# Rings of tiles that rest for some slots before they are taken again, stores a slot later, and more tiles behind them, in a four-layer kernel

## The chip, the cores and the metric

The kernel runs on one core of one Trainium2 chip. The metric is the time of one execution on the device in microseconds (us). All data are float32.

## The reference, cut to what matters

Four images of 384 channels by 48 x 48 positions go through four layers, each on a group-normalised input and added back to it.

```python
x = x + L0(_gn(x), ...)   # in projection, causal convolution, selective scan
                          # (768 channels x 16 states), gate, out projection, layer norm
x = x + L1(_gn(x), ...)   # 1x1 product, 8x8 FFT filter, 3x3 depthwise, gelu gate, 1x1 product
x = x + L2(_gn(x), ...)   # 11x11 depthwise convolution with one kernel per channel
x = x + L3(_gn(x), ...)   # four experts; the routing coefficients come from all four images
...
hdn = relu(einsum('bchw,edc->ebdhw', x, w1) + b1)   # L3
y = einsum('ebdhw,eod->ebohw', hdn, w2) + b2
out = einsum('ebohw,ebhw->bohw', y, coef)
```

## The kernel before, in words

The spine of the program is the scan of layer 0, written out as a fixed order of **slots**. Each image has 480 slots, four images make 1,920, and each slot holds one scan instruction of 460 or 464 positions on DVE (line 966). The scan of slot u needs a decay from ACT (942), a drive `bu = u * B` from POOL (953) and is followed by a product with `C` on DVE (986) or on POOL (995); PE turns the products and adds them up (886). `B` and `C` are rows that SP broadcasts from DRAM to 128 partitions (`spread`, 930): one `B` and one `C` for every two slots, into three and four tiles, so that a broadcast for a later pair of slots is queued only some five slots ahead of its first reader.

Everything else is cut into **tasks**: Python generators that stop at each `yield` and say on what kind of engine the next step runs. In each slot, `Lane.step` goes over the active tasks of a lane in three phases (`act`; then `pe`, `dve`, `pool`; then `late`) and lets each advance by one step at most. What a step emits stands at that place in the fixed order of its engine's queue. A `pe` step also has a weight, and a meter of PE time per slot holds steps back. There are four lanes: `aux` (layer 0's own projections, gates, the residual and the next chunk's load), `start` (layer 0's z of images 2 and 3, made early, during image 0), `one` (layers 1 and 2 and the router's scores of the image before: `later`), `two` (the experts of layer 3: `experts`). `later(b)` starts at slot 42 of image b+1, and `experts(b)` only when `later(b)` and `experts(b-1)` have ended. What is left of the experts of image 2, and layers 1 to 3 of image 3, follow after the last scan; `all_experts` (lines 1850 and 1867) ends the program.

A **ring** (`Ring`) mirrors a pool of n tiles in this order: `take` gives the next tile, `done` marks one as free, and a step that needs a tile isn't emitted until the one n takes before is marked. Where a tile is stored by a DMA, the program marks it when the store is *queued*. The tile framework adds the true dependency: a load into that tile waits on SP until the store has landed. SP issues its DMAs strictly in the order of the program, so all that is queued behind a waiting DMA on SP, the broadcasts of `B` and `C` too, waits as well.

An expert block (144 positions, one of four experts) runs so: `load3` (1737, 1740) queues the loads of `xe`, and for experts 1 to 3 of the running sum `ye`, then lets three slots pass; `block` then has the steps hidden product `ph` (PE), relu `hr` (ACT), second product `pout` (PE), sum (DVE, 1782 or 1785), and the store (1791) one slot after the sum. For expert 0 the sum is put into the `xe` tile and stored from there. In the scans there are two `xe`, two `ye`, one `hr` and one tile of weights; after the scans 3, 3, 3 and 2. In layer 2, `windows` adds a band's sum to the tile `xb`, of which there are two, and stores it (1582) a slot later; `load_band` (1513) fetches the next one.

Of the kernel before, what the change touches and what calls it, by code (L numbers as in the profile page):

```python
# [16 lines left out]
P = 128  # L17
# [11 lines left out]
NE = 4  # L29
# [12 lines left out]


class Ring:


    def __init__(self, make, n):
        self.make, self.n, self.read = make, n, []

    def free(self, k=1):  # L50
        return all(self.read[: max(0, len(self.read) + k - self.n)])

# [5 lines left out]
    def done(self, k):  # L58
        self.read[k] = True

# [34 lines left out]
class Lane:  # L95
# [6 lines left out]

    def step(self, phase, slot, at=0):
        for task in self.active:
            if task.ended:
                continue
            kind, weight, ring, when = task.next
            if PHASE.get(kind, 1) != phase or task.after > slot:
                continue
            if weight and self.bound and self.meter.value + weight > self.meter.limit:  # L110
                continue
            if (ring and not ring[0].free(ring[1])) or (when and not when()):
                continue
            self.meter.value += weight
            task.move(slot)
        self.active = [t for t in self.active if not t.ended]
        while (
            self.queue and len(self.active) < self.width and self.queue[0].at <= max(at, slot)
            and all(t.ended for t in self.queue[0].needs)
        ):  # L120
            task = self.queue.pop(0)
            task.move()
            if not task.ended:
                self.active.append(task)
# [18 lines left out]
def tile_layers(ctx: ExitStack, tc: tile.TileContext, a: dict, out: bass.AP):  # L143
# [21 lines left out]
    gsel = const("gsel", [P, CT, GROUPS], per_channel(a["c_gsel"]))  # L165
    gexp = const("gexp", [GROUPS, C], a["c_gexp"])
    neghalf = cp.tile([P, TT], F32, name="neghalf")
# [7 lines left out]
    def group_norm(st, bank, mean, rstd, name):  # L175

        mv = small.tile([P, CT, 2], F32, name=f"mv{name}", tag="mv")
        for ct in range(CT):
            nc.vector.bn_aggr(mv[:, ct, :], st[:, ct].rearrange("p k s -> p (k s)"))

        def to_groups(src, n, what):
            ps = bank(f"g{what}{name}")
            for ct in range(CT):
                nc.tensor.matmul(
                    ps[:GROUPS, :n], lhsT=gsel[:, ct, :], rhs=src(ct),
                    start=ct == 0, stop=ct == CT - 1,
                )
            return ps[:GROUPS, :n]

        def to_channels(src, n, what):  # L190
            ps = bank(f"c{what}{name}")
            for ct in range(CT):
                nc.tensor.matmul(
                    ps[:, n * ct : n * ct + n], lhsT=gexp[:, bass.ts(ct, P)], rhs=src,
                    start=True, stop=True,
                )
            return ps[:, : n * CT]

        grp = small.tile([GROUPS, 2], F32, name=f"grp{name}", tag="grp")
        nc.vector.tensor_copy(grp, to_groups(lambda ct: mv[:, ct, :], 2, "m"))  # L200
        nc.vector.tensor_copy(mean, to_channels(grp[:, 0:1], 1, "m"))
        dev = small.tile([P, CT], F32, name=f"dev{name}", tag="dev")
        nc.vector.tensor_sub(dev, mv[:, :, 0], mean)
        nc.vector.tensor_mul(dev, dev, dev)
        var = small.tile([GROUPS, 1], F32, name=f"var{name}", tag="var")
        nc.vector.scalar_tensor_tensor(
            var, to_groups(lambda ct: dev[:, ct : ct + 1], 1, "v"), GN_EPS, grp[:, 1:2],
            ALU.add, ALU.add,
        )
        nc.gpsimd.tensor_tensor(var, var, neghalf[:GROUPS, 0:1], ALU.pow)  # L210
        nc.vector.tensor_copy(rstd, to_channels(var, 1, "v"))

    def group_norm_steps(st, ring, mean, rstd, name):
# [15 lines left out]
        def to_channels(src, n, what):  # L229
            ps, k = ring.take(f"c{what}{name}")  # L230
            for ct in range(CT):
                nc.tensor.matmul(
                    ps[:, n * ct : n * ct + n], lhsT=gexp[:, bass.ts(ct, P)], rhs=src,
                    start=True, stop=True,
                )
            return ps[:, : n * CT], k
# [179 lines left out]
    with ExitStack() as first:  # L416
# [54 lines left out]

        stats0 = wp.tile([P, 2, CT, 2, 3, 6], F32, name="stats0")
        mean0 = wp.tile([P, NB, CT], F32, name="mean0")
# [85 lines left out]
        def scans(wk, mm, ring, meter, place, lanes, begin):  # L559
# [9 lines left out]
            def image_stats(b, ct, h):  # L569
# [4 lines left out]
                for k in range(3):  # L574
                    yield ("dve",)
                    nc.vector.bn_stats(stats0[:, b % 2, ct, h, k, :], t[:, bass.ts(k, LB)])

            def image_norm(b):
                yield from group_norm_steps(
                    stats0[:, b % 2].rearrange("p c h k s -> p c (h k) s"), ring,  # L580
                    mean0[:, b], rstd0[:, b], f"0_{b}",
                )
# [54 lines left out]
            def early_z(b, t, j):  # L637
# [21 lines left out]
                ring.done(r)  # L659
                yield ("pool",)  # L660
                nc.sync.dma_start(zd[b][bass.ts(j, P), bass.ds(starts[t], n)], z[:, :n])
# [514 lines left out]
            for tag, shape, n in (  # L1176
# [6 lines left out]
                    ),  # L1183
                    n,
                )
# [82 lines left out]
        def later(b, ring, accr):  # L1268
# [10 lines left out]

            def slots(tag, shape, n):  # L1280

                return Ring(
                    lambda name: d["wk"].tile(shape, F32, name=name, tag=tag, bufs=n), n
                )
# [10 lines left out]
            def begin1():  # L1295
                wk = d["wk"] = stack.enter_context(tc.tile_pool(name=f"l1_{b}", bufs=2))
                d["w_in"] = wk.tile([P, CT, C], F32, name=f"w_in1_{b}", tag="w_in", bufs=1)
                nc.sync.dma_start(d["w_in"], per_channel(a["L1_w_inT"]))
                w = d["w_out"] = wk.tile([P, 2, C], F32, name=f"w_out1_{b}", tag="w_out", bufs=1)
                nc.sync.dma_start(w[:, 0, :], a["L1_w_outT"][:P, :])  # L1300
                nc.sync.dma_start(w[64:P, 1, :], a["L1_w_outT"][P:, :])
                mean = small.tile([P, CT], F32, name=f"mean1_{b}", tag="mean")
# [90 lines left out]
            def finish_strip(hb):  # L1393
# [46 lines left out]
                for ct in range(CT):  # L1440
                    yield ("pe", 1.3, (ring, 1))
                    ps, r = ring.take(f"pb{b}_{hb}_{ct}")
                    nc.tensor.matmul(  # L1443
                        ps[:, :LB], lhsT=w[:, 0, bass.ts(ct, P)], rhs=act[:, 0, :],
                        start=True, stop=False,
                    )
                    nc.tensor.matmul(  # L1447
                        ps[:, :LB], lhsT=w[64:P, 1, bass.ts(ct, P)], rhs=act[64:P, 1, :],
                        start=False, stop=True,
# [27 lines left out]
            x2s = slots("x2", [P, BR * W], 4)  # L1477
            xbs = slots("xb", [P, max(BANDS) * W], 2)
            reps = slots("rep", [P, NBC, NP, BR, BC], 2)
# [67 lines left out]
            def windows(ct, k, r, first, last, final):  # L1547
# [26 lines left out]
                if last:  # L1574
# [5 lines left out]
                    nc.vector.bn_stats(stats3[b % 2][:, ct, k, :], x[:, :n])  # L1580
                    yield ("pool",)
                    nc.sync.dma_start(x3d[b][of_band(ct, k)], x[:, :n])
# [38 lines left out]

            xg = slots("xg", [P, CT, LB], 2)

# [64 lines left out]
        def experts(b, ring, rings):  # L1688
# [42 lines left out]
            def load3(s, e):  # L1731
                yield (
                    "pool", 0, None,
                    lambda: rings["xe"].free() and (not e or rings["ye"].free()),
                )
                x = take(("x", s, e), "xe", f"xe{b}_{s}_{e}")
                nc.sync.dma_start(x, strip(x3d[b], bass.ts(s, EB)))
                if e:
                    y = take(("y", s, e), "ye", f"ye{b}_{s}_{e}")
                    nc.sync.dma_start(y, strip(y3d, bass.ts(s, EB)))  # L1740
                yield from wait(3)

            def block(s, e):
# [33 lines left out]
                yield ("late",)  # L1777
                key = ("y" if e else "x", s, e)
                x = d[key][0]
                if e:  # L1780
                    y = x.rearrange("p c t -> p (c t)")
                    nc.vector.tensor_add(y, ps[:, : CT * EB], y)  # L1782
                else:
                    for m in range(CT):
                        nc.vector.scalar_tensor_tensor(
                            x[:, m, :], ps[:, bass.ts(m, EB)], b2_sum[:, m : m + 1],
                            x[:, m, :], ALU.add, ALU.add,
                        )
                ring.done(r)
                yield ("pool",)  # L1790
                nc.sync.dma_start(strip(out[b] if e == NE - 1 else y3d, bass.ts(s, EB)), x)
                done(key)

# [104 lines left out]

        def of_experts(pool, sizes):
            for tag, n in sizes.items():  # L1900
# [4 lines left out]
                    ),  # L1905
                    n,
                )
# [13 lines left out]
        def begin(b):  # L1921
# [9 lines left out]
            first.enter_context(tc.tile_pool(name="experts", bufs=2)),  # L1931
            {"we": 1, "xe": 2, "ye": 2, "hr": 1},
        )
        with (
# [6 lines left out]
            at = place[0]  # L1941
            while not all(ring.read):
                at += 1
# [5 lines left out]
        with (  # L1949
# [3 lines left out]
            holder[0], ring.n, accr.n = mm, 6, 2  # L1953
            of_experts(wk, {"we": 2, "xe": 3, "ye": 3, "hr": 3})

# [129 lines left out]
```

## Time and profile before

| | |
|---|---|
| median of 3 runs | 5400.23 us (5399.6 to 5402.55) |
| the profiled execution | 5405.14 us, span 5403.1 us |
| mean granted PE clock | 0.919 |
| PE, DVE, POOL, ACT busy | 86%, 75%, 62%, 55% |
| scans of layer 0 | about 85 to 4,512 us |
| rest of the experts of image 2, layers 1 and 2 of image 3 | about 4,512 to 5,060 us |
| scores and all experts of image 3 | about 5,060 to 5,403 us |

In the views, `<-` in the name of a group stands between what is written and what is read. In the waits, each line names who waited, for whom, the total in us, how often, and the longest. `SPq` is the issuing queue of SP: its waits are the times for which a DMA at the head of that queue held it.

### The profile page before, as it was taken

The page shows a single profiled execution, that of the slowest core. Times are in us where ns is not written, and L with a number is a line of the kernel's source. Part 1 is how long each engine was busy: PE and PEld are TensorE (multiplying, and loading weights), DVE is VectorE, ACT ScalarE, POOL GpSimd, SP SyncE. Part 2 cuts the span into 40 slices and gives each one's busy share as a digit, 9 for nine tenths or more (in the row PEclk, how much of TensorE's full clock was granted, in tenths as well). Part 3 has the DMA queues.
Part 4 walks back from the last instruction along what each step waited for, and adds up shares of the span by engine and source line. Part 5 has one row for each costly group of instructions (what it writes and reads, how often), then busy time and mean ns, then how long its engine had stood idle before and what let it go on. Part 6 is the DMA issues. An engine that isn't in the chain of part 4 may idle for free. (4 is left out here: it accounts for less than half of the span.)

```text
span 5403.1 us, 82006 instructions
## 1 busy us (share of the span) xinstructions
PE 4646.1 (86%) x27796; PEld 3666.7 (68%) x27796; DVE 4067.1 (75%) x5581; ACT 2989.0 (55%) x6632; POOL 3363.1 (62%) x3020
## 2 busy tenths in 40 slices
PE   5898877787768988888889988888799988999899
PEld 3555545454446766765668867665678877889799
DVE  5998899889997888889887778798987875452200
ACT  3566655565547765565567745565477653335321
POOL 3788778886677788876678678775677783000000
PEclk8898987788879999998899999998899999999899
DMA  4565545443344555655566565655566573543210
GB/s 152 172 187 175 178 128 150 129 143 120 111 127 131 148 165 157 191 161 147 149 172 178 161 200 155 173 146 149 154 182 174 158 213 115 175 138 105 64 27 23
DMA packets 648873, 794.36 MB, mean 147 GB/s; under 512 B 60149, under 2 KB 642661, under 8 KB 648062
## 3 DMA queue, kind: packets, MB, share of 16 engines
q1 hardware_dynamic: 638148, 787.38, 49.9%
q8 instruction: 221, 3.62, 0.3%
q10 hardware_dynamic: 10298, 1.67, 0.2%
q14 instruction: 206, 1.69, 0.1%
HBM read 685.04 MB, written 103.81 MB: 146 GB/s over the span
## 5 line engine op out<-in xcount | busy, mean ns | idle before, releaser
L953 POOL TENSOR_TENSOR bu<-u,B 128x460 f32<-128x460 f32 (+1 forms) x1920 | 2227.0, 1170 | 795.5 <-DVE g L966 349.8
L942 ACT ACTIVATE da<-dt,a_neg 128x460 f32<-128x460 f32 (+1 forms) x1920 | 1242.4, 648 | 310.6 <-DVE g L986 185.6
L886 PE MATMUL y<-ident,g 128*115 128x128 f32 (+1 forms) x7680 | 1111.3, 292 | 192.5 <-DVE g L986 114.8
L886 PEld LDWEIGHTS y<-ident,g 128*115 128x115 f32 (+1 forms) x7680 | 991.2, 183 | 400.4 <-DVE g L986 140.5
L995 POOL TENSOR_TENSOR g<-g,C 128x460 f32<-128x460 f32 (+1 forms) x885 | 1030.0, 1164 | 246.8 <-ACT carry L980 244.3
L966 DVE TENSOR_TENSOR_SCAN da<-da,carry,bu 128x460 f32<-128x460 f32 (+1 forms) x828 | 971.7, 1174 | 122.2 <-ACT da L942 76.7
L966 DVE TENSOR_TENSOR_SCAN g<-da,carry,bu 128x460 f32<-128x460 f32 (+1 forms) x708 | 819.8, 1167 | 57.7 <-issue 18.8
L986 DVE TENSOR_TENSOR g<-da,C 128x460 f32<-128x460 f32 (+1 forms) x1035 | 656.4, 634 | 175.7 <-DMA C<-bcd 62.0
L980 ACT COPY carry<-da 128x1 f32<-128x1 f32 x828 | 130.3, 157 | 760.5 <-DVE g L986 758.0
L1750 PE MATMUL pout<-hr,we 128*128 128x144 f32 x3456 | 485.0, 297 | 51.5 <-ACT hr L1766 37.8
L1750 PE MATMUL ph<-xe,we 128*128 128x144 f32 x3456 | 484.7, 298 | 33.6 <-DMA xe<-x3d 18.9
L1750 PEld LDWEIGHTS pout<-hr,we 128*128 128x128 f32 x3456 | 456.3, 197 | 75.3 <-ACT hr L1766 47.9
L1750 PEld LDWEIGHTS ph<-xe,we 128*128 128x128 f32 x3456 | 459.4, 199 | 51.5 <-DMA xe<-x3d 13.7
L1557 PE MATMUL pc<-band,row 128*128 128x162 f32 (+14 forms) x3456 | 451.3, 284 | 11.2 <-ACT row L1544 10.9
L1557 PEld LDWEIGHTS pc<-band,row 128*128 128x128 f32 x3456 | 440.0, 194 | 16.6 <-ACT row L1544 11.9
L749 PE MATMUL pin<-xch,w_inx 128*128 128x463 f32 (+2 forms) x720 | 344.8, 621 | 55.1 <-DMA xch<-in_x 32.3
L1415 DVE SCALAR_TENSOR_TENSOR dw<-pad,w_dw,dw 128x384 f32<-128x384 f32 x576 | 348.0, 615 | 20.4 <-ACT pad L1390 9.6
L1037 PE MATMUL po<-w_out,zs 128*115 128x384 f32 (+1 forms) x960 | 342.2, 499 | 14.7 <-DVE ye L1782 9.3
L1766 ACT ACTIVATE hr<-ph,nb 128x144 f32<-128x144 f32 x576 | 176.2, 376 | 279.2 <-PE ph L1750 278.4
L1524 ACT ACTIVATE rep<-x,br,wr 128x192 f32<-128x192 f32 x576 | 273.7, 540 | 4.2 <-issue 4.2
L768 DVE SCALAR_TENSOR_TENSOR xc<-pin,conv_w,xc 128x460 f32<-128x460 f32 (+1 forms) x360 | 249.2, 692 | 30.7 <-ACT xc L762 18.5
L749 PEld LDWEIGHTS pin<-xch,w_inx 128*128 128x128 f32 x720 | 143.8, 213 | 179.8 <-issue 136.3
(211 smaller groups left out, 5979.2 us busy)
## 6 DMA issues: line engine op xcount, KB each, us to landing
B<-bcd SPq DMA_DIRECT2D x768, 230.0 KB, 3.6
C<-bcd SPq DMA_DIRECT2D x768, 230.0 KB, 4.0
B<-bcd SPq DMA_DIRECT2D x192, 232.0 KB, 3.8
C<-bcd SPq DMA_DIRECT2D x192, 232.0 KB, 4.3
xe<-x3d SPq DMA_DIRECT2D x192, 216.0 KB, 2.8
ye<-y3d SPq DMA_DIRECT2D x144, 216.0 KB, 2.8
y3d<-ye SPq DMA_DIRECT2D x96, 216.0 KB, 2.2
xs<-x1d SPq DMA_DIRECT2D x24, 576.0 KB, 5.2
```

The lines of the kernel that those rows point to most:

```text
L749: nc.tensor.matmul(ps[:, lo : halo + n], lhsT=w_inx[:, k, bass.ts(j, P)], rhs=c["x"][:, k, lo : halo + n], start=k == 0, stop=k == CT - 1,)
L886: nc.tensor.matmul(c["y", m][:w, bass.ts(k, P)], lhsT=src[:, bass.ts(k, w)], rhs=ident, is_transpose=True, start=c["terms", m] == 1 and k ...
L942: nc.scalar.activation(da[:, :n], c["dt", p][:, m % 2, :n], AF.Exp, scale=a_neg[:, m, s : s + 1])
L953: nc.gpsimd.tensor_mul(bu[:, :n], c["u", p][:, m % 2, :n], live["B", u // 2][:, :n])
L966: nc.vector.tensor_tensor_scan(here[:, :n], da[:, :n], bu[:, :n], last if t else nil[:, 0:1], ALU.mult, ALU.add,)
L986: nc.vector.tensor_mul(live["g", u][:, :n], live["h", u][:, :n], live["C", u // 2][:, :n])
L995: nc.gpsimd.tensor_mul(g[:, :n], g[:, :n], live["C", u // 2][:, :n])
L1037: nc.tensor.matmul(ps[:w, :C], lhsT=c["zs"][:, m, bass.ts(k, w)], rhs=w_out0[:, m, :], start=m == 0, stop=m == MT - 1,)
L1415: nc.vector.scalar_tensor_tensor(v, src, w_dw[:, ct, k : k + 1], v, ALU.mult, ALU.add)
L1524: nc.scalar.activation(rep[:, :, n, :, :].rearrange("p g r c -> p r g c"), rows.rearrange("p (r g c) -> p r g c", r=BR, c=BC), AF.Identity ...
L1557: nc.tensor.matmul(d["acc2"][0][:, : BANDS[k] * W].rearrange("p (h w) -> p h w", w=W)[:, lo - edges[k] : hi - edges[k], xlo:xhi], lhsT=d[" ...
L1750: nc.tensor.matmul(ps[:, bass.ts(m, EB)], lhsT=w[:, k, bass.ts(m, P)], rhs=of[:, k, :], start=k == 0, stop=k == CT - 1,)
```

## The change

- `Ring` gets a number of slots, `rest`: a tile counts as free only `rest` slots after its `done`. The slot is kept in `CLOCK`, set by every `Lane.step`. The psum rings and most others rest for 0 slots.
- The experts' rings in the scans: `xe` 2 tiles resting 1 slot, `ye` three tiles (two before) resting 2. After the scans the sizes stay 3 and 3, without a rest.
- The sum of expert 0 goes to a `ye` tile and is stored from there; `load3` takes a `ye` for expert 0 too and lets two slots pass, not three. The experts' store is queued two slots after the sum, not one.
- Layer 2: `xb` 4 tiles resting 2 slots (2 tiles before), the store two slots after the sum. The scores' `xg` rest 1 slot.
- The early z: all its rings rest 2 slots, the store comes two slots after the copy.
- Room for the tiles: one `stats0` in place of two; the second part of layer 1's `w_out` (64 rows) moves into the unused partitions of the constant `gexp`, loaded once on ACT's queue instead of once per image on SP.
- In place stay the store of layer 0's residual (1095), the load of its next chunk (731) and the store of layer 1 (1457).

```diff
-    def __init__(self, make, n):
-        self.make, self.n, self.read = make, n, []
+    def __init__(self, make, n, rest=0):
+        self.make, self.n, self.read, self.rest = make, n, [], rest
     def free(self, k=1):
-        return all(self.read[: max(0, len(self.read) + k - self.n)])
+        return all(
+            v is not False and v + self.rest <= CLOCK[0]
+            for v in self.read[: max(0, len(self.read) + k - self.n)]
+        )
...
     def done(self, k):
-        self.read[k] = True
+        self.read[k] = CLOCK[0]
...
     def step(self, phase, slot, at=0):
+        CLOCK[0] = slot
...
-    gexp = const("gexp", [GROUPS, C], a["c_gexp"])
+    gexp = cp.tile([P, C], F32, name="gexp")
+    nc.sync.dma_start(gexp[:GROUPS, :], a["c_gexp"])
+    nc.scalar.dma_start(gexp[64:P, :], a["L1_w_outT"][P:, :])
...
# early_z
-                yield ("pool",)
+                yield from wait(2)
                 nc.sync.dma_start(zd[b][bass.ts(j, P), bass.ds(starts[t], n)], z[:, :n])
...
# later
-                nc.sync.dma_start(w[:, 0, :], a["L1_w_outT"][:P, :])
-                nc.sync.dma_start(w[64:P, 1, :], a["L1_w_outT"][P:, :])
+                nc.sync.dma_start(w, a["L1_w_outT"][:P, :])
...
-            xbs = slots("xb", [P, max(BANDS) * W], 2)
+            xbs = slots("xb", [P, max(BANDS) * W], 4, 2)
...
# windows
-                    yield ("pool",)
+                    yield from wait(2)
                     nc.sync.dma_start(x3d[b][of_band(ct, k)], x[:, :n])
...
-            xg = slots("xg", [P, CT, LB], 2)
+            xg = slots("xg", [P, CT, LB], 2, 1)
...
# experts: load3
-                    lambda: rings["xe"].free() and (not e or rings["ye"].free()),
+                    lambda: rings["xe"].free() and rings["ye"].free(),
...
+                y = take(("y", s, e), "ye", f"ye{b}_{s}_{e}")
                 if e:
-                    y = take(("y", s, e), "ye", f"ye{b}_{s}_{e}")
                     nc.sync.dma_start(y, strip(y3d, bass.ts(s, EB)))
-                yield from wait(3)
+                yield from wait(2)
...
# experts: block, expert 0
                         nc.vector.scalar_tensor_tensor(
-                            x[:, m, :], ps[:, bass.ts(m, EB)], b2_sum[:, m : m + 1],
+                            y[:, m, :], ps[:, bass.ts(m, EB)], b2_sum[:, m : m + 1],
                             x[:, m, :], ALU.add, ALU.add,
                         )
+                    done(("x", s, e))
                 ring.done(r)
-                yield ("pool",)
-                nc.sync.dma_start(strip(out[b] if e == NE - 1 else y3d, bass.ts(s, EB)), x)
-                done(key)
+                yield from wait(2)
+                nc.sync.dma_start(strip(out[b] if e == NE - 1 else y3d, bass.ts(s, EB)), y)
+                done(("y", s, e))
...
-            {"we": 1, "xe": 2, "ye": 2, "hr": 1},
+            {"we": 1, "xe": 2, "ye": 3, "hr": 1}, {"xe": 1, "ye": 2},
...
-            while not all(ring.read):
+            while not ring.free(ring.n):
```

More of the change, by code (lines that the diff above doesn't have):

```diff
@@ L41 @@
 LN_EPS = 1e-5
+CLOCK = [0]
 class Ring:
-    def __init__(self, make, n):
-        self.make, self.n, self.read = make, n, []
+    def __init__(self, make, n, rest=0):
+        self.make, self.n, self.read, self.rest = make, n, [], rest
     def free(self, k=1):
-        return all(self.read[: max(0, len(self.read) + k - self.n)])
+        return all(
+            v is not False and v + self.rest <= CLOCK[0]
+            for v in self.read[: max(0, len(self.read) + k - self.n)]
+        )
     def take(self, name):
@@ L193, in to_channels @@
                 nc.tensor.matmul(
-                    ps[:, n * ct : n * ct + n], lhsT=gexp[:, bass.ts(ct, P)], rhs=src,
+                    ps[:, n * ct : n * ct + n], lhsT=gexp[:GROUPS, bass.ts(ct, P)], rhs=src,
                     start=True, stop=True,
@@ L232, in to_channels @@
                 nc.tensor.matmul(
-                    ps[:, n * ct : n * ct + n], lhsT=gexp[:, bass.ts(ct, P)], rhs=src,
+                    ps[:, n * ct : n * ct + n], lhsT=gexp[:GROUPS, bass.ts(ct, P)], rhs=src,
                     start=True, stop=True,
@@ L470, in tile_layers @@
         nc.vector.tensor_reduce(b2_sum, b2_all.rearrange("p e c -> p c e"), AX.X, ALU.add)
-        stats0 = wp.tile([P, 2, CT, 2, 3, 6], F32, name="stats0")
+        stats0 = wp.tile([P, 1, CT, 2, 3, 6], F32, name="stats0")
         mean0 = wp.tile([P, NB, CT], F32, name="mean0")
@@ L575, in image_stats @@
                     yield ("dve",)
-                    nc.vector.bn_stats(stats0[:, b % 2, ct, h, k, :], t[:, bass.ts(k, LB)])
+                    nc.vector.bn_stats(stats0[:, 0, ct, h, k, :], t[:, bass.ts(k, LB)])
             def image_norm(b):
                 yield from group_norm_steps(
-                    stats0[:, b % 2].rearrange("p c h k s -> p c (h k) s"), ring,
+                    stats0[:, 0].rearrange("p c h k s -> p c (h k) s"), ring,
                     mean0[:, b], rstd0[:, b], f"0_{b}",
@@ L1183, in scans @@
                     ),
-                    n,
+                    n, 2,
                 )
@@ L1278, in put, with slots @@
                 tasks.append(task)
-            def slots(tag, shape, n):
+            def slots(tag, shape, n, rest=0):
                 return Ring(
-                    lambda name: d["wk"].tile(shape, F32, name=name, tag=tag, bufs=n), n
+                    lambda name: d["wk"].tile(shape, F32, name=name, tag=tag, bufs=n), n, rest
                 )
@@ L1298, in begin1 @@
                 nc.sync.dma_start(d["w_in"], per_channel(a["L1_w_inT"]))
-                w = d["w_out"] = wk.tile([P, 2, C], F32, name=f"w_out1_{b}", tag="w_out", bufs=1)
-                nc.sync.dma_start(w[:, 0, :], a["L1_w_outT"][:P, :])
-                nc.sync.dma_start(w[64:P, 1, :], a["L1_w_outT"][P:, :])
+                w = d["w_out"] = wk.tile([P, C], F32, name=f"w_out1_{b}", tag="w_out", bufs=1)
+                nc.sync.dma_start(w, a["L1_w_outT"][:P, :])
                 mean = small.tile([P, CT], F32, name=f"mean1_{b}", tag="mean")
@@ L1443, in finish_strip @@
                     nc.tensor.matmul(
-                        ps[:, :LB], lhsT=w[:, 0, bass.ts(ct, P)], rhs=act[:, 0, :],
+                        ps[:, :LB], lhsT=w[:, bass.ts(ct, P)], rhs=act[:, 0, :],
                         start=True, stop=False,
@@ L1447, in finish_strip @@
                     nc.tensor.matmul(
-                        ps[:, :LB], lhsT=w[64:P, 1, bass.ts(ct, P)], rhs=act[64:P, 1, :],
+                        ps[:, :LB], lhsT=gexp[64:P, bass.ts(ct, P)], rhs=act[64:P, 1, :],
                         start=False, stop=True,
@@ L1777, in block @@
                 yield ("late",)
-                key = ("y" if e else "x", s, e)
-                x = d[key][0]
+                y = d["y", s, e][0]
                 if e:
-                    y = x.rearrange("p c t -> p (c t)")
-                    nc.vector.tensor_add(y, ps[:, : CT * EB], y)
+                    of = y.rearrange("p c t -> p (c t)")
+                    nc.vector.tensor_add(of, ps[:, : CT * EB], of)
                 else:
@@ L1897, in tile_layers, with of_experts @@
         place = [0]
-        def of_experts(pool, sizes):
+        def of_experts(pool, sizes, rest):
             for tag, n in sizes.items():
@@ L1905, in of_experts @@
                     ),
-                    n,
+                    n, rest.get(tag, 0),
                 )
@@ L1953, in tile_layers @@
             holder[0], ring.n, accr.n = mm, 6, 2
-            of_experts(wk, {"we": 2, "xe": 3, "ye": 3, "hr": 3})
+            of_experts(wk, {"we": 2, "xe": 3, "ye": 3, "hr": 3}, {})
             one.queue += later(NB - 1, ring, accr)
```

## The prediction

> **What bounds the kernel now.** I read the page first, then SP's own waits, then DVE's waits, then the issuing queue of SP row by row, then engine times by stage. By the page no engine is the bound of the whole (PE 86%, DVE 75%), so the stages decide.
>
> SP's own waits (who, at which line, for what: total us, times, longest) show what the change is about:
>
> ```profile
> SPq L930 <- POOL bu L953: 1759.8, 649, 12.1
> ...
> SPq L1740 <- DMA y3d<-ye: 244.6, 92, 7.5
> SPq L1791 <- DVE ye L1782: 240.2, 91, 7.6
> SPq L1737 <- DMA y3d<-xe: 156.8, 47, 8.0
> SPq L1513 <- DMA x3d<-xb: 139.0, 52, 5.6
> SPq L1582 <- DVE xb L1578: 116.4, 43, 8.0
> SPq L1740 <- DMA out<-ye: 113.9, 39, 7.2
> ```
>
> The first line is the normal state: a broadcast of B waits until POOL has read the tile, so SP is in step. Lines 1740, 1737 and 1513 are loads into a tile whose store was queued just before and has not landed: 244.6 + 113.9 + 156.8 + 139.0 = 654 us of SP. Lines 1791 and 1582 are stores queued before DVE has made the sum. Who pays? DVE's and POOL's waits:
>
> ```profile
> DVE g L986 <- DMA C<-bcd: 62.0, 28, 6.1
> ...
> POOL bu L953 <- DMA B<-bcd: 98.2, 49, 7.2
> ```
>
> So of 654 us little reaches an engine: a broadcast is queued some five slots ahead. It does where the experts run beside bare scans; SP's queue there (start, duration):
>
> ```profile
> 4387.29 0.39 SPq L1791 DMA_DIRECT2D out<-ye  x1
> 4387.77 0.43 SPq L1737 DMA_DIRECT2D xe<-x3d  x1
> 4393.64 0.36 SPq L1740 DMA_DIRECT2D ye<-y3d  x1
> 4394.09 0.44 SPq L930 DMA_DIRECT2D B<-bcd  x1
> ...
> 4397.58 0.56 SPq L1737 DMA_DIRECT2D xe<-x3d  x1
> 4403.03 0.36 SPq L1740 DMA_DIRECT2D ye<-y3d  x1
> 4403.48 0.44 SPq L930 DMA_DIRECT2D B<-bcd  x1
> ```
>
> Each block the queue stands still for 5 us (4388.20 to 4393.64, 4398.14 to 4403.03), waiting for the store that it has just sent; then two pairs of broadcasts go out together, late. DVE's product at 4400.39 and that at 4409.31 each wait 1.67 us for C.
>
> By stage (us, busy PE, PEld, DVE, ACT, POOL, clock, DMA):
>
> ```profile
> 2080.00:2154.00 74.00, 67.11 (x484) 57.79 (x483) 64.19 (x91) 43.20 (x76) 60.02 (x54) 1.00 0.57 150
> 2700.00:2760.00 60.00, 48.23 (x319) 38.76 (x317) 56.75 (x84) 34.87 (x81) 44.34 (x41) 0.97 0.59 171
> 2880.00:2940.00 60.00, 59.02 (x428) 51.56 (x427) 46.10 (x58) 45.96 (x114) 47.61 (x43) 1.00 0.62 185
> 4600.00:4800.00 200.00, 197.03 (x1259) 167.15 (x1260) 101.89 (x188) 73.15 (x168) 0.77 (x4) 0.98 0.52 153
> ```
>
> Row 1, experts beside bare scans: nothing is full. Row 2, layer 1 beside experts: DVE 95%, so SP's waits cost next to nothing. Row 3, layer 2 beside experts: PE 98%. Row 4, after the scans: PE 98%, and each expert block still to do costs its own PE time.
>
> **A: SP's waits in the scans.** DVE's idle time ended by C is 62.0. POOL's waits for B pass to DVE in part: the view of tile B has 27.5 and 13.1 us of scans waiting behind them, 40.6. Sum 102.6. For each of these waits I took SP's rows of the 12 us before it and the longest standstill other than a broadcast's. For C: 28.1 us behind the ye load, 9.1 behind the xb load, 7.8 behind the xe load, so 45 of 62; 14.6 behind the next chunk's load (731), which stays. For B, 88% of POOL's waits stand behind these three loads: 36 of 40.6. Removable: 81 us. How much is realised? Bounds: 0 (PE or DVE takes the place at once) and 81. Most of the waits lie in stages like rows 1 and 3, half of which are full on PE; I take 40.
>
> Is a rest of two slots enough? A slot is 2.3 us (4,425 us of scans over 1,920), so two are 4.6. The DMA table gives a landing after 2.2 us for y3d<-ye and 4.5 for out<-ye, and the waits go up to 7.5. The Trainium skill ("DMA: Bandwidth & Descriptors", Anatomy of one DMA) has about 2.0 us fixed plus bytes over 436e3 per us: for the 221,184 bytes here an estimate of 2.5 us. By the page a rest of two slots covers every store and A's 81 us are all removable; by the trace out<-ye (48 of 144 ye stores) lands at the edge, and a part of its wait stays. The trace decides, another reason to take 40. The same section says that a DMA's semaphore wait happens on the issuing sequencer, as the rows above show; xe and xb rest or have two more tiles, so these should go to near zero.
>
> **B: the pace of the experts.** Before, an expert's ye (xe for expert 0) is held for 8 slots: load, three of wait, ph, relu, pout, sum, store, next take. Two tiles give a block every 4 slots; the trace agrees (y3d<-xe stores at 2131.34, 2140.29, 2148.04 and 2154.80, 7.8 us apart; 2.3 us x 4 is 9.2 at the mean slot, and these slots are shorter). After: load at 0, ph 3, pout 5, sum 6, store 8, free 10: three tiles give 3.33; for expert 0 xe is free at 7, two tiles give 3.5. The floor of hr is 3. So 12 to 17% faster where latency sets the pace; elsewhere the PE meter does.
>
> But experts(b) waits for later(b) too. The last scores of image 2 are loaded at 4372, the experts of image 1 end with a store at 4451, some 33 slots later (counted by scans). later becomes longer: a band's last window ends a slot later and the next band's first needs it, 15 bands, 15 slots, and some 3 for xg's rest. So the experts of image 2 can start at most 33 - 18 = 15 slots sooner, about 4 blocks at 3.5, plus one from the faster pace up to the scans' end: 5 blocks leave the tail. There a block costs 2 x 2.21 = 4.4 us (the chain has ph and pout at 2.21 for 18 matmuls). In the scans it costs what slots with experts take above slots with only scores: slots 864 to 912 took 88 us, 912 to 960 took 111; 0.48 us a slot, 1.9 a block. Gain 5 x (4.4 - 1.9) = 12. Bounds: 0, and 25 if the longer layer 2 costs no slot.
>
> **C: between the last scan and the tail** (4506 to 4590) expert 0's chain is store 4.2, xe load 2.7, ph, pout, sum. The store leaves it. PE was idle 3.0 of 60 and 11.7 of 60 us in the two rows from 4500; at most 15, I take 6.
>
> **D: what costs.** ph comes three slots after its load, not four: 2.3 us less lead. The load lands in 2.8 median, 9.1 at most; PE and its loader wait 18.9 and 20.7 us for xe now, and as the standstills that delay it go, I add 3 (0 to 15). The early z takes one slot more per task; 60 of them in a row fill 690 - 200 = 490 us now, 60 slots more end near 820, before their limit at slot 480 (1047 us): 0; SP's waits for the copy before that store (104 us) reach an engine with 2.3 + 2.6 us for C and B between 150 and 1100, so they give 3 at most. The w_out rows: one DMA more on ACT's queue at the start, 0.4 us, four fewer on SP. stats0: image 1's statistics come long after image 0's were used. Stores later on SP move past at most one pair of broadcasts and their neighbours; whoever waits for them (y3d, 16 blocks later; x3d for the scores, after the last band) is far, but for the last band, one slot.
>
> Sum: -40 - 12 - 6 + 3 = -55. Of the profiled execution, 5405.1 (its span and 2.0 around it): 5350. It stood 4.9 above the median, so 5345 for the median.
>
> **The rivals.** (1) *Slower: layer 2's extra slots.* If lane one loses more than the 33 slots of slack (18 by my count, the rest because experts that are ready more often take meter time from layers 1 and 2), the experts of image 2 start later than before, and each 3.5 slots push a block of 4.4 us into a tail that is 98% PE. At 60 slots: 27 / 3.5 = 8 blocks, +34 us, less 10 from A: 5424. For it: the meter is shared, and row 3 is full. Against: lane one is served first. (2) *No change:* A goes to PE and DVE at once (rows 2 and 3), B is eaten by layer 2: 5397. For it: of SP's 654 us at the three loads 81 reach DVE, an eighth. (3) *More:* all 81 are realised, B and C at their ends: 5405 - 81 - 25 - 15 - 5 = 5279. For it: in row 1 no engine is full, and SP's loop of store, landing, load is the only thing that repeats. (4) *It doesn't do what it says:* the stores land later than two slots and ye loads still stand: A 15 instead of 40, 5370; in the range.
>
> **How the numbers follow.** Main case with (4) 0.57, (3) 0.13, (2) 0.12, (1) 0.18. 0.2% is 11 us, about what a measurement can tell from no change. Faster 0.70, same 0.12, slower 0.18. The main case alone spans 5310 to 5385; with (3) and most of (1) the range is 5272 to 5424.
>
> **What would show it.** Right: SP's lines for 1740, 1737 and 1513 waiting for stores fall from 654 to below 150 us; DVE's waits for C from 62 to near 25 (the chunk's load remains); y3d stores of expert 0 every 3.5 slots; the last scan 40 to 50 us earlier, the tail 12 to 20 us shorter. Wrong: a last scan at the same time with these waits gone (rival 2), or later(2) ending after slot 1,890 and more than 59 blocks after the scans (rival 1).

## The result, and the profile after

The changed kernel takes 5353.4 us against 5399.9 (medians of 4 runs each): ratio 0.9917, 95% interval 0.990 to 0.9934. It is 46 us faster, where the prediction had 55. Its profiled execution took 5354.36 us, with a span of 5352.2. The lines of the code moved by 10 or 11: SP's broadcasts are now at line 941, `load3` at 1747 and 1750, the experts' store at 1801, xb's load and store at 1523 and 1592, the scan at 977, the product with C at 997.

SP's own waits in the changed kernel (who, where, for what: total us, times, longest):

```profile
SPq L941 <- POOL bu L964: 2376.2, 823, 11.8
...
SPq L1747 <- PE ph L1760: 153.3, 63, 9.2
SPq L1801 <- DVE ye L1791: 144.8, 74, 8.2
...
SPq L1592 <- DVE xb L1588: 67.5, 29, 10.8
...
SPq L1750 <- DMA y3d<-ye: 64.0, 37, 5.9
...
SPq L1750 <- DMA out<-ye: 19.9, 17, 2.9
...
SPq L1523 <- DMA x3d<-xb: 17.8, 11, 3.0
```

Loads that stand behind a store still under way cost SP 64.0 + 19.9 + 17.8 = 102 us, where they had cost 654, and SP waits longer in its normal state (first line, 1,760 before). Two stretches of its queue (start, duration). The first is from expert 3 of image 1, as the rows of before are, though beside the last scores and not beside bare scans; the second from expert 0 of image 2 beside bare scans, where a block loads no `ye`:

```profile
4331.02 0.44 SPq L1801 DMA_DIRECT2D out<-ye  x1
4332.70 0.33 SPq L941 DMA_DIRECT2D B<-bcd  x1
...
4333.56 0.42 SPq L1747 DMA_DIRECT2D xe<-x3d  x1
4336.14 0.37 SPq L1750 DMA_DIRECT2D ye<-y3d  x1
...
4447.10 0.37 SPq L1747 DMA_DIRECT2D xe<-x3d  x1
4447.52 0.49 SPq L1801 DMA_DIRECT2D y3d<-ye  x1
4448.45 0.33 SPq L941 DMA_DIRECT2D B<-bcd  x1
```

In the first stretch a load of `ye` still stands 2.2 us behind a store (4333.98 to 4336.14; in the rows of before it was 5), but a pair of broadcasts has gone out in between. In the second no load waits for the store, and a broadcast leaves 0.4 us after it. DVE's waits in the changed kernel:

```profile
DVE da L977 <- ACT da L953: 96.1, 78, 7.6
DVE g L997 <- PE y L897: 64.8, 43, 12.0
DVE da L977 <- ACT carry L991: 47.9, 18, 7.6
...
DVE g L997 <- DMA C<-bcd: 4.2, 3, 2.1
```

C is no cause of idle time any more (62.0 before, 4.2 now), and POOL's waits for B fell from 98.2 to 16.5. But the three lines above it have grown by 21 us together; before, they were:

```profile
DVE da L966 <- ACT da L942: 93.3, 66, 6.4
...
DVE g L986 <- PE y L886: 53.4, 36, 8.9
...
DVE da L966 <- ACT carry L980: 41.0, 16, 5.1
```

The 1,920th scan starts at 4515.3 us before and at 4508.5 after. So of 51 us of span only 7 were won in the scans, and 44 after them. The stretch after the last scan, before (first pair) and after (second pair; window, its length, busy PE, PEld, DVE, ACT, POOL):

```profile
4500.00:4560.00 60.00, 56.98 (x383) 49.09 (x382) 24.60 (x46) 15.98 (x39) 14.71 (x13) 1.00 0.29 81
4560.00:4620.00 60.00, 48.27 (x352) 46.48 (x351) 12.96 (x39) 16.59 (x40) 2.42 (x8) 0.86 0.59 176
```

```profile
4500.00:4560.00 60.00, 58.29 (x396) 50.62 (x395) 18.95 (x41) 15.73 (x39) 9.41 (x10) 1.00 0.34 99
4560.00:4620.00 60.00, 58.19 (x432) 53.40 (x431) 13.31 (x31) 20.11 (x50) 1.16 (x6) 1.00 0.86 268
```

PE's idle time there fell from 14.8 to 3.5 us. And by the last scan 139 of 192 expert blocks have been stored, 134 before.

That the waits for B and C went and yet the scans ended hardly sooner is what the experiments have to explain.

### The profile page after: what moved, and what is told of

It is laid out like the page before. It is cut to its first block, busy times and chain, and to the rows that moved or that the text cites. A ratio compares the mean times of both kernels' runs of the same rounds, so it can differ in the third digit from the quotient of the medians.

```text
span 5352.2 us, 81964 instructions
## 1 busy us (share of the span) xinstructions
PE 4643.7 (87%) x27796; PEld 3663.3 (68%) x27796; DVE 4069.8 (76%) x5581; ACT 2986.2 (56%) x6632; POOL 3363.0 (63%) x3020
## 5 line engine op out<-in xcount | busy, mean ns | idle before, releaser
L977 DVE TENSOR_TENSOR_SCAN da<-da,nil,bu 128x460 f32<-128x460 f32 x207 | 242.4, 1171 | 31.5 <-ACT carry L991 18.9
```

Of the source, the lines that this page charges most:

```text
L977: nc.vector.tensor_tensor_scan(here[:, :n], da[:, :n], bu[:, :n], last if t else nil[:, 0:1], ALU.mult, ALU.add,)
```

## The experiments

All ratios are to the kernel before in the same set of runs, with 95% intervals. "Last scan" is the start of the 1,920th scan on DVE in the profiled execution, "tail" the rest of its span, "blocks" the expert stores by the last scan. One profiled execution can lie up to 18 us from its kernel's median, so the ratio decides and the columns say where.

| kernel | ratio | last scan | tail | blocks |
|---|---|---|---|---|
| before | 1 | 4515 | 888 | 134 |
| changed | 0.9917 (0.990 to 0.9934) | 4508 | 844 | 139 |
| tiles only | 0.9854 (0.984 to 0.9868) | 4444 | 885 | 134 |
| five tiles only | 0.9862 (0.9844 to 0.988) | 4455 | 882 | 134 |
| experts' part only | 0.9868 (0.9854 to 0.9882) | 4482 | 840 | 140 |
| layer 2's part only | 1.0001 (0.9992 to 1.0009) | 4545 | 865 | 138 |
| early z's part only | 0.9997 (0.9988 to 1.0006) | 4521 | 885 | 134 |
| experts' part, xb's tiles | 0.9859 (0.984 to 0.9877) | 4490 | 841 | 140 |
| changed, x3d's store soon | 0.9885 (0.9867 to 0.9903) | 4511 | 838 | 140 |
| changed, experts' store soon | 0.9917 (0.9901 to 0.9933) | 4521 | 854 | 139 |
| changed, experts don't rest | 0.9905 (0.989 to 0.9921) | 4524 | 851 | 139 |
| tiles only, dense at the end | 0.9845 (0.9832 to 0.9859) | 4440 | 872 | 135 |
| experts' part, old pace | 0.9888 (0.9869 to 0.9907) | 4473 | 875 | 133 |
| old pace, dense at the end | 0.9885 (0.9866 to 0.9904) | 4477 | 870 | 135 |

**Tiles only.** The rings count as before, so every engine gets its instructions in the order of before; only the tiles behind them are more (the room comes from `gexp`, `w_out` and `stats0`, as in the change).

```diff
+                both = n == 2 and tag in ("xe", "ye")
                 rings[tag] = Ring(
-                    lambda name, tag=tag, shape=shape, n=n: pool.tile(
+                    lambda name, tag="xy" if both else tag, shape=shape, n=5 if both else n:
+                    pool.tile(shape, F32, name=name, tag=tag, bufs=n),
...
-            xbs = slots("xb", [P, max(BANDS) * W], 2)
+            xbs = slots("xb", [P, max(BANDS) * W], 4)
+            xbs.n = 2
```

> The order of before on every engine, as the rings still count two tiles; but behind the experts' two xe and two ye of the scans stand five tiles in rotation, and four behind xb, so that a load meets a tile whose store was sent a block earlier. Theory S (the standstills of SP were what cost): they go (lines 1740, 1737, 1513 from 654 us to under 150) and the time falls by 35 to 50 us, to about 5355. Theory P (the pace of the experts was: more blocks done before the tail, and no store in the chain after the last scan): the order is unchanged, 134 stores by the last scan as before, and the time falls by 0 to 12 us, to about 5393.

Measured: 0.9854, 79 us faster than before by the ratio, more than both theories and more than the whole change. The waits of SP and DVE:

```profile
SPq L1742 <- DMA y3d<-ye: 58.2, 27, 6.3
...
SPq L1515 <- DMA x3d<-xb: 15.9, 11, 2.0
...
SPq L1742 <- DMA out<-ye: 7.8, 11, 1.8
```

```profile
DVE da L968 <- ACT da L944: 86.7, 62, 6.4
...
DVE g L988 <- PE y L888: 44.1, 33, 8.9
DVE da L968 <- ACT carry L982: 42.7, 18, 5.5
...
DVE g L988 <- DMA C<-bcd: 9.3, 5, 5.7
```

Here the standstills fell as in the changed kernel (to 82 us), C's line nearly went, and nothing rose in its place: of the other three lines two are shorter than before. The last scan comes 71 us sooner, with the same 134 blocks by then, and the tail is 3 us shorter. So the standstills did cost the scans some 71 us. The order is the same but for four small loads of weights that leave SP to make room, and these are worth nothing: layer 2's part and the early z's part below have the same edits for room, at ratios of 1.0001 and 0.9997.

The 71 us lie near the ceiling of 81 that the prediction gave, but they did not come by its two paths alone. By the records, DVE's idle time for a DMA fell by 50 us, that for PE by 17, and that for POOL by 4.5 where the prediction counted 36. PE itself had waited for loads that stood in SP's queue; the prediction's sum had this path for `xe` as a cost of 3 us, and for `xch`, the next chunk's input, not at all. Before, then with the tiles alone:

```profile
PE pin L749 <- DMA xch<-in_x: 32.3, 10, 6.3
PE ph L1750 <- DMA xe<-x3d: 18.9, 15, 2.6
```

```profile
PE pin L751 <- DMA xch<-in_x: 12.6, 9, 3.5
...
PE ph L1752 <- DMA xe<-x3d: 3.4, 6, 0.9
```

**The three parts, one at a time**, each put into before with its edits of the change, and with those that make room for the tiles (`gexp`, `w_out`, `stats0`):

> Before with the experts' part of the change alone (three ye, rests, expert 0 in ye, store two slots after the sum, load's wait of two). S: about three quarters of the standstills go, -30 us, 5370. P: the slots before the tail are won without layer 2 becoming longer: at least the whole gain of the change, -45 to -55 us, 5350; some 140 stores by the last scan.

> Before with layer 2's part alone (four xb resting two slots, store two slots after the sum, xg resting one). S: the standstills at xb go (139 us of SP, 9 us of DVE's waits for C), -5 to -10 us, 5392. P: later ends some 15 slots later, the experts' start is not yet bound by it (slack 33), 0 to +8 us, 5404.

> Before with the early z's part alone. S: -3 us. P: nothing of the experts changes; the changed kernel's scans of image 0 were 4 to 7 us later than before, so if the early z causes that, +4 us at slot 480, and 5400 to 5406 in all.

Measured: 0.9868, 1.0001 and 0.9997. The experts' part alone is better than the whole, and than either theory had it. Its scans end 33 us sooner and its tail is 48 us shorter. Layer 2's part alone gives nothing: in its profile the scans end 30 us later and the tail is 23 us shorter. So the parts do not add up: one by one they give 1.3% and twice nothing, together 0.8%. The early z's part took SP's waits for ACT at that store from 104 to 15 us and left the time where it was: those waits were free. The changed kernel's 4 us at slot 480 are not shown to be its effect: kernels that leave the early z alone (tiles only, layer 2's part) show 6 and 8 us there too, the experts' part 2.

**Is the gain that is given back given by layer 2 or by the experts' order?** The experts' part with xb's tiles under an unchanged ring of two (as in "tiles only"):

> Before with the experts' part of the change, and for layer 2 only the tiles: four behind xb while the ring counts two, so that layer 2 keeps its order. Theory T (the standstills cost some 75 us of scans, and the change gives half of it back by the order of its layer 2): below the experts' part alone by what xb's standstills cost, 10 us, ratio 0.983 to 0.985. Rival U (what is given back comes from the experts' denser order): no better than the experts' part alone, 0.987, and worse than the tiles alone, 0.985.

And the tiles without xb's:

> The order of before, five tiles in rotation behind the experts' two xe and two ye, xb as before. By the share of xb among the waits for B and C that stood behind loads (21 of 126 us) xb's tiles carry an eighth to a sixth: T and U both give 0.987 (some 10 us more than with xb's tiles too); if it is 0.985 again, xb's standstills cost nothing; if above 0.990, they carry a third or more.

Measured: 0.9859 and 0.9862. Sparing SP the landing of x3d on top gives 0.1%, twice, which the intervals cannot tell from nothing: xb's standstills cost little, if anything. And the experts' part does not come near the sum of "tiles only" and its own shorter tail. With all of these standstills gone, its scans end at 4490 instead of 4444, and its tail is 44 us shorter: it moves time from the tail into the scans, and against the tiles alone (0.9854) it neither wins nor loses. Rival U is right in that the denser order makes the scans dearer, but this costs nothing in sum. What the changed kernel (0.9917) lacks to this one, 0.6% or some 31 us, must come with the rest of its edits: layer 2's part and the early z.

The changed kernel with layer 2's store one slot after the sum:

```diff
-                    yield from wait(2)
+                    yield ("pool",)
                     nc.sync.dma_start(x3d[b][of_band(ct, k)], x[:, :n])
```

> The changed kernel with layer 2's store one slot after the sum again (four xb resting two slots stay). T, in the form that the late store's 15 slots make layer 2 longer and its stages dearer: 15 to 25 us of the loss return, ratio 0.987 to 0.989. U: as the changed kernel, 0.991 to 0.992.

Measured: 0.9885, as T had it: 0.3%, some 17 us, of the change's loss go with layer 2's late store, by intervals that just touch, so this is likely and not shown beyond doubt. In the stage of layer 2 of image 1 (slots 1186 to 1378) the profiled executions took 459 us before, 475 changed, 455 with the store soon; other stages gave it back in this one execution (its scans end at 4511), so where the 17 us lie is not known. Put into before, the whole of layer 2's part cost nothing (1.0001): if its late store costs here, it does so only together with the experts' part.

**Store and rest of the experts, in the changed kernel.** The store one slot after the sum:

> The changed kernel with the experts' store one slot after the sum again (a ye is held for 9 slots with its rest, three tiles give a block every 3 slots, the floor of hr). T: SP waits for the sum some 100 us more, which no engine sees, and the pace is a little faster: 0.990 to 0.993. Rival: the late store is what keeps SP moving; then some 20 us are lost, 0.995.

No rests (`{}` in place of `{"xe": 1, "ye": 2}`):

> The changed kernel with the experts' rings resting 0 slots (three ye, expert 0 in ye, late store stay). If the rest is what spares SP the landing: ye loads stand again behind the store queued in the same slot, 150 us or more at that line (84 in the changed kernel), DVE's waits for C come back in part, 0.994 to 1.000. If three tiles suffice by themselves, 0.990 to 0.993.

Measured: 0.9917 and 0.9905, both as the changed kernel. Without rests the standstills came back in part, with the waits for C:

```profile
SPq L1750 <- DMA y3d<-ye: 160.8, 56, 5.7
...
SPq L1750 <- DMA out<-ye: 59.8, 26, 7.4
```

```profile
DVE g L997 <- DMA C<-bcd: 24.8, 11, 6.4
```

and the time didn't move, though the profiled execution, from which these lines come, was the slowest of four. In the order of the changed kernel 221 us of SP and 25 us of DVE decide nothing that these runs can measure; something else sets its pace. The first half of the expectation (lines come back) was right, its time was not. The rests and the late store of the experts, each taken away by itself, bring nothing measurable beside three tiles.

**The tiles, and a denser end.** The tiles alone, with a ring of four xe from slot 1888 on (`if u == N - PAIR: rings["xe"].n = 4`):

> The tiles alone (order of before, five tiles in rotation), but from slot 1888 on, when expert 0 of image 2 runs beside bare scans and later beside nothing, the ring of xe counts four. If the order of before is the better one only where layers 1 and 2 compete, and a denser order pays at the end (the experts' part alone had a tail 48 us shorter than before, 6 blocks of it from the scans), another 10 to 25 us go: 0.981 to 0.984. If the tail of the experts' part came from its order in the tail itself, as the tiles alone: 0.985 to 0.986.

Measured: 0.9845, the fastest of all; its interval overlaps that of the tiles alone, so the extra 5 us or so are not shown. One block more than with the tiles alone by the last scan, and three more at 4,600 us (157 against 154).

**The experts' pace.** The experts' part with xb's tiles and longer rests (`{"xe": 2, "ye": 4}`), so that a block takes at least four slots, as before; and the same with the short rests from slot 1856 on:

> The experts' part with xb's tiles (ratio 0.986), but with longer rests, xe 2 and ye 4 slots: an expert block at most every 4 slots, as before. Theory V (the faster pace of the experts moves cost from the tail into the scans and is worth nothing in sum; the standstills are all of the gain): scans end some 30 us earlier than with the fast pace (near 4450 against 4485), about 134 blocks by then, the tail longer by as much: 0.984 to 0.987. Rival W (the pace pays: 6 blocks of 4.4 us): 0.988 to 0.991. Rival X (the later store and load's shorter wait, not the pace, make the scans dearer): scans end near 4485 again and the tail is longer, 0.989 or more.

> The same, but from slot 1856 on with the rests of the change (1 and 2 slots), so that only the end is dense. V: 5 to 15 us below it. X and W: as it.

Measured: 0.9888 and 0.9885. Against the fast pace (0.9859) the scans end 17 us sooner and the tail is 34 us longer: the pace pays, some 16 us, as W had it, by intervals that just overlap. But at the old pace, with 133 blocks, the scans still end at 4473, 29 us after those of "tiles only". What is left between these two is the form of the experts' part: the sum of expert 0 in ye, the store two slots after the sum, a load's wait of two slots, and the rests. Which of them makes the scans dearer was not tried here; the store and the rests, tried in the changed kernel, moved nothing.

## Why the prediction was right, and where its sum was not

- **SP's standstills go.** Predicted: from 654 to below 150 us; measured 102. DVE's waits for C: predicted near 25, measured 4.2. The part behind the next chunk's load, which was to stay, went too, though SP still waits 67.1 us there (72.8 before). Rival 4, stores landing later than the rest, is out. Of the two sides weighed there, the estimate of 2.5 us from the Trainium skill ("DMA: Bandwidth & Descriptors", Anatomy of one DMA) would have left no wait, the trace's longer landings a part. That section fits its figures to DMAs issued by GpSimd, and these stores are issued by SP, so the trace was rightly preferred: a single wait still lasts up to 5.9 us, but all of them are a sixth of what they were.
- **A, sized 40 us.** This term failed twice, in opposite directions. The standstills cost 71 us (tiles only), so halving 81 because PE or DVE takes the place was too cautious; but the 71 came in part through PE and not through POOL, so that they lie near 81 does not confirm how the 81 were put together. And of the 71 the changed kernel kept 7 in its scans: the order that came with it made the scans dearer, a price for which the prediction had no term beyond 1.9 us for each of 5 blocks and 3 us for ph. By its own sum the scans were to gain 40 - 10 - 3 = 27 us; its sign of being right, a last scan 40 to 50 us earlier and a tail 12 to 20 us shorter, does not follow from this sum, and it was 7 and 44.
- **Where the price sits.** Slots 923 to 1378 took 1115 us before, 1094 with the tiles alone and 1132 in the changed kernel; slots 1482 to 1857 took 953, 928 and 945. In these, layers 1 and 2 compete with the experts. Only beside bare scans (1378 to 1482: 236, 215, 223) did the change get most of what was there. DVE's idle time within the scans, as far as the records put it down to another engine or a DMA, says the same: 502 us before, of which 62 for DMA; 431 with the tiles; 488 changed, where of the 57 us less for DMA 48 are eaten by 36 us more for ACT and 12 more for PE.
- **B, five blocks.** Right in its count: 134 to 139 by the last scan, and the first store of the experts of image 2 at slot 1883 instead of 1899, 16 slots sooner where the sum had at most 15. Its two terms were off: counted by scans, 36 slots and not 33 lay between the last scores of image 2 and the end of the experts of image 1, and these scores were loaded 8 slots later, not 18. Expert 0's first ten stores of image 0 are 6.9 us apart instead of 9.1, 3.6 slots instead of 4.3 (predicted 3.5).
- **B and C, the tail.** Sized 12 net of the blocks' cost in the scans, and 6. The tail became 44 us shorter: 5 blocks of 4.4 us are 22, PE's idle time just after the scans 11 (C's ceiling was 15), which leaves 11 without a name. Before the blocks' cost in the scans is taken off, the prediction had 22 and 6 here, 28 us. The old pace confirms the mechanism: the tail grows by 34 us, with 7 blocks fewer done, when the pace goes. The cost of a block in the scans was misread: slots 864 to 912 of before took 96 us and the next 48 took 104, not 88 and 111, so a block costs 0.6 us there by that way of reckoning and not 1.9.
- **The rivals.** Rival 1, layer 2's extra slots, has a true part: the late store likely costs some 17 us, half of the 34 given. But the experts' start was not pushed past its slack (it came 16 slots sooner), so the point from which it was to decide was not the one. Layer 2's lane does seem to have taken over the start, though: the experts of image 1 end 32 slots sooner (slot 1855 instead of 1887), and the first store of image 2 comes 28 slots after that, where it came 12 after before. Rival 2 describes what became of the scans (A was taken up elsewhere), for another reason: not a full engine but another order. Rival 3's first term, all 81 us of the standstills, is what the tiles alone nearly reach (71).
- **D.** PE's waits for `xe`, put at 3 us more, are gone from the views of the changed kernel instead (18.9 us before). The early z and the start show no cost that a run here can separate.

The total came out because two misses met: the scans gained 7 us where the sum has 27, the rest of the program 44 where it has 28. That they nearly cancelled is luck. The two mechanisms are there, the standstills that go and the blocks that leave the tail, but in this kernel the first paid almost nothing net, and the second and what came with it paid nearly everything.

What stays open: which part of the experts' form costs the scans the 29 us, why layer 2's late store costs nothing by itself, and whether xb's ring of four, xg's rest and the early z together take the 0.26% between the changed kernel with x3d's store soon (0.9885) and the experts' part with xb's tiles (0.9859), whose intervals meet.

## What to carry to other kernels

Where an in-order DMA queue reloads a tile right behind its store, everything queued after the load waits for the landing too; more tiles in rotation take that away without touching a schedule. Do this first with the order of all instructions unchanged, and measure it by itself: here that was worth 1.5%, more than the redesign that also moved the stores (0.8%), and it showed that the redesign's new order gave the rest back. A removed wait is booked as a gain only once it is known that the order that removes it doesn't put another engine last instead, as ACT and PE came last here.

## What the runs showed of the hardware that had not been expected

Standstills of 654 us on SP, of which DVE's records showed 62 us as waits for C, were worth 71 us of scans; 104 us of SP's waits at the early z were worth nothing, and 139 at xb some 0.1% or nothing. And 221 us of the same standstills, brought back in the changed kernel by taking the rests away, were worth nothing that could be measured. How long the queue stalled did not decide whether it cost time: the longest single one was 8.0 us at xe, 7.5 at ye, 7.2 at the early z and 5.6 at xb. That it is the lead of the next broadcast over its reader that decides is the likely reading, but no run here measured it.
